# Spreading the p row by a VectorE transpose and DRAM instead of TensorE, with a reordered head and one GpSimd scaling at the end

## The chip, the cores and the metric

The kernel runs on one core of one Trainium2 chip. The metric is device time in microseconds (us), the median of repeated executions.

## The reference, cut to what matters

For each of 16 samples, x is 1024 x 256 (f32) and adj is a symmetric 0/1 matrix of 1024 x 1024 (int32). Two layers follow each other.

```
# layer 0: sigmoid attention on the edges, then residual and layer norm
e     = leaky(einsum('id,jd->ij', x * a0, x))          # symmetric in i, j
alpha = where(adj == 1, sigmoid(e), 0)
x     = layernorm(x + alpha @ x + bias)
# layer 1: exp attention on the edges, then residual and layer norm
H     = x @ W
s, d  = H @ a_src, H @ a_dst
e     = where(adj != 0, exp(-leaky(s[:, None] + d[None, :])), 0)
x     = layernorm(x + elu((e @ H) / rowsum(e)))
```

The reference also covers edge values 2 to 4; the kernel checks that there are none and has a general path behind that check, which these inputs do not take.

## The kernel before

All 16 samples go through one pass, `one_kind_pass`, sample b in slot b. A sample's 1024 rows are 8 tiles of 128. All matrix products are f32. An edge weight of layer 1 is min(adj, p[n] * q[m]) with p = exp(-0.8 s) and q = exp(-0.8 d), up to factors that are put into H and cancel in the division by the row sum. So the weights tile of row block m needs q as one number per partition and **p as a row of 1024 numbers that is the same on all 128 partitions**. `project` leaves p and q as columns (`pqs[b]`, tile number along the free axis); something has to turn p into rows.

The order of instructions on every engine is written out by hand (`tc.manual_schedule()`), so each engine runs its list in program order. A slot b, from 1 on, has three stretches on TensorE:

- strips (about 22 us): `strip(b, jt)`, scores of tile jt against the tiles from jt on (matmul L227), two tanh on ScalarE (L235, L236), their maximum on VectorE (L237); `finish` (L243, and a diagonal addition on GpSimd, L253), and the mirror images through DRAM (`dump` L259/L263, `gather` L267, `mask` L274). In between lie the projections of sample b - 1 (`project`, L405; exps on ScalarE L413 and L414, H on L415). At jt = 6 comes `share_p(b-1)`: p's columns are transposed by TensorE (L431), copied to SBUF by ScalarE (L433), written to a DRAM row (L435) and read back to all partitions (L437), both DMAs from GpSimd's queue.
- sum0 (about 28 us): `multiply0` (L342), 8 tiles of 16 matmuls; after each tile `end0` on VectorE (L352, L295, L297), and, at t = 2 to 7, ahead of that tile's `end0`, the weights of sample b - 1 (`weights`, L449): tiles 0 and 1 at t = 2, one each at t = 3 to 6, two at t = 7.
- sum1 (about 28 us): `sum1` (L456) for sample b - 1, 8 tiles of 16 matmuls; VectorE and ScalarE end each tile (`elu` L479 to L489, `add` L494 to L297).

The last sample has no later slot to hide in. Its projections are laid between the tiles of sum1 of sample 14, after t = 5 and after t = 6, and each half of p is spread by four TensorE transposes and a ScalarE copy (`spread_p`, L424, L425). Its first four sum1 tiles run side by side over m while its weights are made; the other tiles follow, the last one in two halves of its columns (L715). The layer norm of the last tiles ends the program; `scale1` (L325) applies it to tiles 3 to 5 on ScalarE, which also loads the table for a square root there (L666).

At the head, x of sample 0 comes in four pieces of two tiles (L94, from the queues of SyncE and ScalarE in turn), and GpSimd's queue issues adj of sample 0 in four pieces (L102; two row halves, first for columns 0 to 511), then x and adj of sample 1. `transpose_x` (L203) turns each piece of x by TensorE; VectorE and ScalarE copy it out and scale it (L207 to L211). Then come strips 0 and 1, each in two chunks of columns, `finish` and `mirror` (L282, L284), and sum0.

Of the kernel before, what the change touches and what calls it, by code (L numbers as in the profile page):

```python
# [18 lines left out]
P = 128  # L19
# [11 lines left out]
def one_kind_pass(  # L31
# [64 lines left out]
    def load_adj(b, g, columns=None):  # L96

        if (b, g) not in adjs:
            adjs[b, g] = two.tile([P, HT, N], BF16, tag=f"adj{g}", name=f"adj_{b}_{g}")
        columns = columns or slice(None)  # L100
        rows = adjT[b].rearrange("(t p) i -> p t i", p=P)[:, ts(g, HT), columns]
        nc.gpsimd.dma_start(adjs[b, g][:, :, columns], rows)  # L102
# [62 lines left out]
    pcol = ps_e.tile([P, HALF], F32, tag="e", name="pcol")[:, 0:ND]  # L165
    nc.tensor.transpose(pcol, arow, ident[0:ND, 0:ND])
    nc.scalar.copy(acol, pcol)
    power = const.tile([P, NT], F32, tag="power", name="power")
    nc.gpsimd.memset(power, -0.5)
    def make_Wx(c):  # L170
# [4 lines left out]
            nc.vector.tensor_reduce(Wx[:, c, s : s + 1], wprod, AX.X, ALU.add)  # L175


    xTs, xas, als, tbs, mirs = {}, {}, {}, {}, {}

    def new_xT(b):  # L180

# [12 lines left out]
    def transpose_x(b, g):  # L194

        if g == 0:
            new_xT(b)
            xas[b] = one.tile([P, ND, N], F32, tag="xa", name=f"xa_{b}")
        for c in range(ND):
            pool, tag = ((ps_t, "t"), (ps_acc, "acc"), (ps_acc if c else ps_e, "acc" if c else "e"), (ps_t, "t"))[g]  # L200
            pt = pool.tile([P, 2, P], F32, tag=tag, name=f"pxT_{b}_{g}_{c}")
            for t in range(2):
                nc.tensor.transpose(pt[:, t, :], xs[b][:, 2 * g + t, ts(c, P)], ident)  # L203
            flat = pt.rearrange("p t q -> p (t q)")
            xT, xa = xTs[b][:, c, ts(g, 2 * P)], xas[b][:, c, ts(g, 2 * P)]
            if c == 0:
                nc.vector.tensor_copy(xT, flat)  # L207
                nc.vector.tensor_scalar(xa, xT, acol[:, 0:1], None, ALU.mult)
            else:
                nc.scalar.copy(xT, flat)  # L210
                nc.scalar.mul(xa, flat, acol[:, 1:2])  # L211

    def strip(b, jt):


        if jt == 0:
            als[b] = one.tile([P, NT, N], F32, tag="al", name=f"al_{b}")
        width = N - jt * P
        tb = four.tile([P, N], F32, tag="tb", name=f"tb_{b}_{jt}")
        tbs[b, jt] = tb  # L220
        n_chunks = -(-width // HALF)
        per = -(-(width // P) // n_chunks) * P
        for n, o in enumerate(range(0, width, per)):
            w = min(per, width - o)
            pe = ps_e.tile([P, HALF], F32, tag="e", name=f"pe_{b}_{jt}_{n}")
            for c in range(ND):
                nc.tensor.matmul(  # L227
                    pe[:, 0:w],
                    lhsT=xTs[b][:, c, ts(jt, P)],
                    rhs=xas[b][:, c, ds(jt * P + o, w)],  # L230
                    start=(c == 0),
                    stop=(c == ND - 1),
                )
            low = two.tile([P, HALF], F32, tag="low", name=f"low_{b}_{jt}_{n}")
            nc.scalar.activation(tb[:, ds(o, w)], pe[:, 0:w], AF.Tanh, scale=0.5)  # L235
            nc.scalar.activation(low[:, 0:w], pe[:, 0:w], AF.Tanh, scale=0.5 * SLOPE)  # L236
            nc.vector.tensor_tensor(tb[:, ds(o, w)], tb[:, ds(o, w)], low[:, 0:w], ALU.max)  # L237

    def finish(b, jt, c0=0, c1=N):

# [150 lines left out]
    def project(b, t):  # L391

        if t == 0:
            if b < B - 1:
                H = one.tile([P, NT, D + 1], F32, tag="H", name=f"H_{b}")
                Hs[b] = [H[:, m, :] for m in range(NT)]
            else:
                Hs[b] = []
                for g in range(2):
                    H = two.tile([P, HT, D + 1], F32, tag=f"adj{g}", name=f"H_{b}_{g}")  # L400
                    Hs[b] += [H[:, m, :] for m in range(HT)]
            pqs[b] = small.tile([P, NT, 2], F32, tag="pq", name=f"pq_{b}")
# [11 lines left out]
        nc.scalar.activation(pqs[b][:, t, :], pt[:, 0:2], AF.Exp, scale=SLOPE - 1.0)  # L414
        nc.scalar.mul(Hs[b][t][:, 0:D], pt[:, 2:], w)  # L415

    def spread_p(b, g):

        if g == 0:
            p_bcs[b] = one.tile([P, N], F32, tag="p", name=f"p_{b}")  # L420
        pt = ps_t.tile([P, HT, P], F32, tag="t", name=f"pp_{b}_{g}")
        for t in range(HT):
            col = pqs[b][:, g * HT + t, 0:1]
            nc.tensor.transpose(pt[:, t, :], col.to_broadcast([P, P]), ident)  # L424
        nc.scalar.copy(p_bcs[b][:, ts(g, HALF)], pt.rearrange("p t q -> p (t q)"))  # L425

    def share_p(b):


        pt = ps_t.tile([P, HT, P], F32, tag="t", name=f"prow_{b}")[0:NT, 0, :]  # L430
        nc.tensor.transpose(pt, pqs[b][:, :, 0], ident)  # L431
        row = one.tile([NT, P], F32, tag="row", name=f"row_{b}")
        nc.scalar.copy(row, pt)  # L433
        p_row = dram.tile([N], F32, tag="p_row", name=f"p_row_{b}")
        nc.gpsimd.dma_start(p_row.rearrange("(t p) -> t p", p=P), row)  # L435
        p_bcs[b] = one.tile([P, N], F32, tag="p", name=f"p_{b}")
        nc.gpsimd.dma_start(p_bcs[b], p_row.partition_broadcast(P))  # L437

    def check_pq(b):
        near = small.tile([P, NT, 2], F32, tag="near", name=f"near_{b}")  # L440
# [4 lines left out]
    def weights(b, m):  # L445

        if m == 0:
            es[b] = one.tile([P, NT, N], F32, tag="ew" if b < B - 1 else "al", name=f"e_{b}")
        nc.vector.scalar_tensor_tensor(  # L449
            es[b][:, m, :], p_bcs[b], pqs[b][:, m, 1:2], adjs[b, m // HT][:, m % HT, :], ALU.mult, ALU.min  # L450
        )

    hs, ys, y_of, mv1s, r1s = {}, {}, {}, {}, {}

# [48 lines left out]
    def scale1(b, t):  # L503
        scale(ys[b][t], *r1s[b][t])
# [8 lines left out]

    for g in range(NT // 2):
        transpose_x(0, g)
    bias_bc = const.tile([P, D], F32, tag="bias", name="bias_bc")

    nc.vector.memset(bias_bc[:, 0:1], 0.0)  # L520
# [4 lines left out]
    nc.sync.dma_start(a_bc, a[0].partition_broadcast(P))  # L525
    Wx = const.tile([P, ND, D + 2], F32, tag="Wx", name="Wx")
    nc.sync.dma_start(Wx[:, :, 2:], W.rearrange("(c p) o -> p c o", p=P))
    strip(0, 0)
    strip(0, 1)
    for jt in range(2):  # L530
        finish(0, jt, 0, HALF)
        mirror(0, jt)
# [30 lines left out]
    for b in range(1, B):  # L563
# [58 lines left out]
        for t in range(NT):  # L622
            acc = acc1(prev, t, ps_acc, "acc")
            for m in range(NT):
                sum1(prev, t, acc, m)
            if last and t == 6:
                turn_x1(b, 1)
            if last and t == 7:
                weights(b, 0)
            elu(prev, t, acc)  # L630
            if last and t == 7:
                for m in range(1, 4):
                    weights(b, m)
            if t >= 1:
                add(prev, t - 1)
            if t == 0:
                fetch_x1(b, 0)
            if t in (1, 2):
                scale0(b, 2 * t + 2)
                scale0(b, 2 * t + 3)  # L640
            if t == 2:
                save_x1(b, 1)
            if t == 4:
                fetch_x1(b, 1)
                turn_x1(b, 0)
            if not last and t in (3, 5):
                turn_x(b + 1, (t - 3) // 2)
            if not last and t == 6:
                turn_x1(b, 1)
            if last and t in (5, 6):  # L650
                for n in range(HT):
                    project(b, (t - 5) * HT + n)
                spread_p(b, t - 5)
        if not last:
            add(prev, NT - 1)
            r1s[prev] = center(mv1s[prev], f"1_{prev}")
# [517 lines left out]
```

## Time and profile before

| | |
|---|---|
| median of 3 runs | 1272.78 us (1272.75 to 1272.94) |
| the profiled execution | 1273.82 us, of which the span in the trace is 1271.7 us |
| granted TensorE clock | 0.999 |
| PE busy | 1261.2 us, 99% of the span |
| DVE busy | 924.9 us, 73% |
| ACT busy | 651.4 us, 51% |
| POOL busy | 293.5 us, 23% |

PE is TensorE's matmuls, PEld its weight loads, DVE VectorE, ACT ScalarE, POOL GpSimd, SP SyncE; L431 is line 431 of the kernel before. The engines' busy times overlap. "out<-in" names the tile written and the tiles read. In the timeline a row is start, length, engine, line, operation, tiles, shape and count; instructions of one group that follow each other are merged into one row. A bracket at its end tells how long the engine was idle before it and on whom it waited. A DMA_DIRECT2D row on a queue is the issue of the transfer, not the transfer.

### The profile page before, as it was taken

The page shows a single profiled execution, that of the slowest core. Times are in us where ns is not written, and L with a number is a line of the kernel's source. Part 1 is how long each engine was busy: PE and PEld are TensorE (multiplying, and loading weights), DVE is VectorE, ACT ScalarE, POOL GpSimd, SP SyncE. Part 2 cuts the span into 40 slices and gives each one's busy share as a digit, 9 for nine tenths or more (in the row PEclk, how much of TensorE's full clock was granted, in tenths as well). Part 3 has the DMA queues.
Part 4 walks back from the last instruction along what each step waited for, and adds up shares of the span by engine and source line. Part 5 has one row for each costly group of instructions (what it writes and reads, how often), then busy time and mean ns, then how long its engine had stood idle before and what let it go on. Part 6 is the DMA issues. An engine that isn't in the chain of part 4 may idle for free.

```text
span 1271.7 us, 17514 instructions
## 1 busy us (share of the span) xinstructions
PE 1261.2 (99%) x5484; PEld 1025.7 (81%) x5484; DVE 924.9 (73%) x2017; ACT 651.4 (51%) x1469; POOL 293.5 (23%) x593
## 2 busy tenths in 40 slices
PE   9999999999999999999999999999999999999997
PEld 6788787887878878788787887878788787887886
DVE  5686867858678686786768868687686867868657
ACT  4644645456454564544645445454455645456434
POOL 2213231212312122121232212223112231212203
PEclk9999999999999999999999999999999999999999
DMA  9388595895949869497695966949579595895312
GB/s 219 67 174 143 103 188 96 176 181 101 194 88 180 168 117 200 77 183 154 130 194 92 182 133 139 209 83 182 117 168 188 95 190 97 174 181 103 99 34 69
DMA packets 603416, 180.24 MB, mean 142 GB/s; under 512 B 481722, under 2 KB 585652, under 8 KB 603316
## 3 DMA queue, kind: packets, MB, share of 16 engines
q1 hardware_dynamic: 581760, 135.85, 54.3%
q0 software_dynamic: 20864, 42.53, 18.6%
q8 instruction: 46, 0.75, 0.3%
q10 hardware_dynamic: 692, 0.66, 0.2%
q14 instruction: 54, 0.44, 0.1%
HBM read 151.91 MB, written 60.62 MB: 167 GB/s over the span
## 4 chain that ended last, share of the span: by engine, by line
PE 98%; DMA 1%; DVE 0%; ACT 0%; issue 0%; ACTq 0%; DVEq 0%
PE acc L342 35%; PE acc L456 35%; PE pe L227 19%; PE pH L405 9%; DMA x<-in_x 1%; PE pal L282 0%; PE prow L431 0%; PE pp L424 0%; ACT y L325 0%; ACT y_kept L325 0%; ACT L666 0%; PE px1T L388 0%; DVE y L494 0%; PE pxT L203 0%; ACTq L136 0%
## 5 line engine op out<-in xcount | busy, mean ns | idle before, releaser
L342 PE MATMUL acc<-x,al 128*128 128x256 f32 x2048 | 445.5, 379 | 0.0
L456 PE MATMUL acc<-H,e 128*128 128x257 f32 x2032 | 445.3, 380 | 0.0
L456 PEld LDWEIGHTS acc<-H,e 128*128 128x128 f32 x2032 | 384.8, 190 | 57.2 <-DVE e L449 0.6
L342 PEld LDWEIGHTS acc<-x,al 128*128 128x128 f32 x2048 | 387.7, 190 | 51.7
L227 PE MATMUL pe<-xa,xT 128*128 128x384 f32 (+1 forms) x720 | 250.9, 486 | 0.0
L227 PEld LDWEIGHTS pe<-xa,xT 128*128 128x128 f32 x720 | 132.7, 189 | 80.8 <-issue 43.1
L325 ACT ACTIVATE x<-x,mr,r 128x256 f32<-128x256 f32 x128 | 69.4, 592 | 227.8 <-POOL mr L321 227.8
L449 DVE SCALAR_TENSOR_TENSOR e<-p,pq,adj 128x1024 f32<-128x1024 f32 x128 | 159.7, 1269 | 29.2 <-DMA p<-p_row 26.1
L304 POOL TENSOR_SCALAR ve<-mv 128x4 f32<-128x4 f32 (+2 forms) x49 | 16.8, 343 | 657.0 <-DVE mv L297 652.9
L488 ACT ACTIVATE h<-acc,rinv 128x256 f32<-128x256 f32 x126 | 59.1, 469 | 203.4 <-DVE rinv L480 187.9
L235 ACT ACTIVATE tb<-pe 128x512 f32<-128x512 f32 (+1 forms) x192 | 94.1, 490 | 119.8 <-PE pe L227 94.6
L479 DVE TENSOR_SCALAR rinv<-acc 128x1 f32<-128x1 f32 x127 | 19.9, 157 | 161.2 <-PE acc L456 161.1
L237 DVE TENSOR_TENSOR tb<-tb,low 128x512 f32<-128x512 f32 (+1 forms) x192 | 103.3, 543 | 39.9 <-ACT low L236 39.8
L125 ACT ACTIVATE junk<-adj,minus 128x2048 bf16<-128x2048 bf16 x64 | 127.3, 1989 | 0.0
L405 PE MATMUL pH<-Wx,x1T 128*128 128x258 f32 x512 | 126.3, 381 | 0.0
L405 PEld LDWEIGHTS pH<-Wx,x1T 128*128 128x128 f32 x512 | 97.2, 190 | 35.8 <-issue 14.3
L253 POOL TENSOR_TENSOR al<-ident,al 128x128 f32<-128x128 f32 x128 | 67.0, 523 | 230.4 <-DVE al L243 229.9
L243 DVE SCALAR_TENSOR_TENSOR al<-tb,adj 128x512 f32<-128x512 f32 (+7 forms) x132 | 97.4, 739 | 5.3 <-DVE tb L237 0.4
L236 ACT ACTIVATE low<-pe 128x512 f32<-128x512 f32 (+1 forms) x192 | 93.2, 485 | 0.5 <-DVE tb L237 0.5
L274 DVE SCALAR_TENSOR_TENSOR al<-al,adj 128x512 f32<-128x512 f32 (+3 forms) x150 | 77.3, 539 | 19.7 <-DMA al<-mir 19.6
L352 DVE SCALAR_TENSOR_TENSOR x<-acc,bias_bc 128x256 f32<-128x256 f32 x128 | 53.7, 420 | 41.5 <-PE acc L342 41.5
L259 DVE STREAM_TRANSPOSE tb<-tb 128x896 f32<-128x896 f32 (+6 forms) x105 | 74.7, 712 | 3.6
(108 smaller groups left out, 950.1 us busy)
## 6 DMA issues: line engine op xcount, KB each, us to landing
adj<-in_adjT POOLq DMA_DIRECT2D x30, 1024.0 KB, 10.3
x_rows<-x SPq DMA_DIRECT2D x31, 512.0 KB, 4.6
x1T<-x_rows SPq DMA_DIRECT2D x248, 64.0 KB, 2.5
out<-y_kept SPq DMA_DIRECT2D x30, 512.0 KB, 6.8
x<-in_x SPq DMA_DIRECT2D x14, 1024.0 KB, 6.1
xT<-in_x SPq DMA_DIRECT2D x112, 128.0 KB, 4.7
p<-p_row POOLq DMA_DIRECT2D x15, 512.0 KB, 4.5
mir<-tb SPq DMA_DIRECT2D x60, 112.0 KB, 3.0
```

The costliest lines, as they stand in the source:

```text
L125: nc.scalar.activation(junk, rows, AF.Square, bias=minus1, scale=2.0, accum_out=chk[:, b * CHECKS + n : b * CHECKS + n + 1],)
L227: nc.tensor.matmul(pe[:, 0:w], lhsT=xTs[b][:, c, ts(jt, P)], rhs=xas[b][:, c, ds(jt * P + o, w)], start=(c == 0), stop=(c == ND - 1),)
L235: nc.scalar.activation(tb[:, ds(o, w)], pe[:, 0:w], AF.Tanh, scale=0.5)
L236: nc.scalar.activation(low[:, 0:w], pe[:, 0:w], AF.Tanh, scale=0.5 * SLOPE)
L237: nc.vector.tensor_tensor(tb[:, ds(o, w)], tb[:, ds(o, w)], low[:, 0:w], ALU.max)
L243: nc.vector.scalar_tensor_tensor(als[b][:, jt, c0:c1], tbs[b, jt][:, c0 - jt * P : c1 - jt * P], 1.0, adjs[b, jt // HT][:, jt % HT, c0:c1] ...
L259: nc.vector.transpose(tb, tb)
L274: nc.vector.scalar_tensor_tensor(v, v, 1.0, rows, ALU.add, ALU.mult)
L342: nc.tensor.matmul(acc, lhsT=als[b][:, jt, ts(t, P)], rhs=xs[b][:, jt, :], start=(jt == 0), stop=(jt == NT - 1),)
L405: nc.tensor.matmul(pt, lhsT=x1Ts[b][:, c, ts(t, P)], rhs=Wx[:, c, :], start=(c == 0), stop=(c == ND - 1),)
L449: nc.vector.scalar_tensor_tensor(es[b][:, m, :], p_bcs[b], pqs[b][:, m, 1:2], adjs[b, m // HT][:, m % HT, :], ALU.mult, ALU.min)
L456: nc.tensor.matmul(acc, lhsT=es[b][:, m, ts(t, P)], rhs=Hs[b][m], start=(m == 0), stop=(m == NT - 1),)
```

## The change

- `spread_p` goes. `share_p` now transposes p's columns on VectorE: p and q live in one constant tile `pq_kept` of 128 x 32 (zeroed once), p in columns 0 to 7 and q in 8 to 15, and VectorE's 32 x 32 block transpose writes `pT`. For samples 0 to 14 one DMA writes all of pT (128 rows of 128 B) to DRAM and one reads it back to all partitions, as four runs of 1 KB for each partition. The p row then has its blocks in the order (i, t, j) in place of (t, i, j).
- `weights` for samples 0 to 14 is therefore four instructions of 128 x 256 for each row block, in place of one of 128 x 1024; the adj and e operands are read and written in runs of 32 elements.
- For sample 15 the projections come after t = 4 and t = 6, its first x1 half is turned at t = 3 in place of t = 4, and p goes through DRAM in halves of 512 columns: for each half four writes of 4 x 128 B and one broadcast. Its weights are made in halves of the columns, the first halves before and between the first four m, the second halves from m = 5 on.
- The first adj DMA is held until the first piece of x has come, by a one-element copy from x into adj's tile on GpSimd.
- At the head, the product of strip 0's first chunk goes between the third and the fourth transposed piece of x; the other chunks' products and tanh steps are reordered.
- The scaling of tile 4 of the last sample goes from ScalarE to GpSimd.

```diff
 # load_adj
             adjs[b, g] = two.tile([P, HT, N], BF16, ...)
+            if (b, g) == (0, 0):
+                nc.gpsimd.tensor_copy(adjs[b, g][:, 0, 0:1], xs[b][:, 0, 0:1])
...
+    pq_kept = const.tile([P, SQ], F32, tag="pq", name="pq_kept")
+    nc.gpsimd.memset(pq_kept, 0.0)
...
 # project
-            pqs[b] = small.tile([P, NT, 2], F32, tag="pq", name=f"pq_{b}")
+            pqs[b] = pq_kept[:, 0 : 2 * NT].rearrange("p (k t) -> p k t", k=2)
...
-    def spread_p(b, g):
...
+    def share_p(b, t0=0, n=NT):
+        if t0 == 0:
+            p_bcs[b] = one.tile([P, P // SQ, NT, SQ] if b < B - 1 else [P, N], F32, ...)
+        pT = one.tile([P, SQ], F32, tag="pT", name=f"pT_{b}_{t0}")
+        nc.vector.transpose(pT, pq_kept)
+        if b < B - 1:
+            p_row = dram.tile([P // SQ, SQ, SQ], F32, tag="p_row", name=f"p_row_{b}")
+            nc.gpsimd.dma_start(p_row.rearrange("i t j -> (i t) j"), pT)
+            nc.gpsimd.dma_start(p_bcs[b], p_row[:, 0:NT, :].partition_broadcast(P))
+        else:
+            p_row = dram.tile([n * P], F32, tag="p_end", name=f"p_row_{b}_{t0}")
+            v = p_row.rearrange("(t i j) -> i t j", i=P // SQ, j=SQ)
+            for i in range(P // SQ):
+                nc.gpsimd.dma_start(v[i], pT[ds(i * SQ + t0, n), :])
+            nc.gpsimd.dma_start(p_bcs[b][:, ds(t0 * P, n * P)], p_row.partition_broadcast(P))
...
 # weights(b, m, t0=0, n=NT), cols = ds(t0 * P, n * P)
-        nc.vector.scalar_tensor_tensor(
-            es[b][:, m, :], p_bcs[b], pqs[b][:, m, 1:2], adjs[b, m // HT][:, m % HT, :], ALU.mult, ALU.min
-        )
+        if b < B - 1:
+            e, rows = [v.rearrange("p (t i j) -> p i t j", i=P // SQ, j=SQ) for v in (e, rows)]
+            for i in range(P // SQ):
+                nc.vector.scalar_tensor_tensor(e[:, i], p_bcs[b][:, i], q, rows[:, i], ALU.mult, ALU.min)
+        else:
+            nc.vector.scalar_tensor_tensor(e, p_bcs[b][:, cols], q, rows, ALU.mult, ALU.min)
...
 # head
-    for g in range(NT // 2):
+    for g in range(3):
         transpose_x(0, g)
+    score(0, 0, 0)
+    transpose_x(0, 3)
...
-    strip(0, 0)
-    strip(0, 1)
+    for jt, n in ((1, 0), (0, 1)):
+        score(0, jt, n)
+    for jt, n in ((0, 0), (1, 0), (0, 1)):
+        squash(0, jt, n)
+    score(0, 1, 1)
+    squash(0, 1, 1)
...
 # sum1 of sample 14, tile t (last), around elu(prev, t, acc)
+            if last and t == 3:
+                turn_x1(b, 0)
             if last and t == 7:
-                weights(b, 0)
+                for m in range(2):
+                    weights(b, m, 0, HT)
             elu(prev, t, acc)
             if last and t == 7:
-                for m in range(1, 4):
-                    weights(b, m)
+                for m in range(2, 6):
+                    weights(b, m, 0, HT)
...
-            if last and t in (5, 6):
+            if last and t in (4, 6):
+                t0 = (t - 4) // 2 * HT
                 for n in range(HT):
-                    project(b, (t - 5) * HT + n)
-                spread_p(b, t - 5)
+                    project(b, t0 + n)
+                share_p(b, t0, HT)
...
 # the first four sum1 tiles of sample 15, step m
-        if m >= 4:
-            weights(last, m)
-        if m == 5:
+        if m in (3, 4):
+            weights(last, m + 3, 0, HT)
+        if m == 4:
             add(done, NT - 1)
             r1s[done] = center(mv1s[done], f"1_{done}")
+        for k in range(3 * m - 15, min(3 * m - 12, NT)) if m >= 5 else []:
+            weights(last, k, HT, HT)
...
 # the end
+    y, (r, mr) = ys[last][4], r1s[last][4]
+    nc.gpsimd.tensor_scalar(y, y, r, mr, ALU.mult, ALU.add)
     scale1(last, 3)
-    scale1(last, 4)
```

`strip` is split into `score` (the matmuls) and `squash` (two tanh and the maximum); in all other places it calls both in the old order.

More of the change, by code (lines that the diff above doesn't have):

```diff
@@ L175, in make_Wx @@
             nc.vector.tensor_reduce(Wx[:, c, s : s + 1], wprod, AX.X, ALU.add)
-    xTs, xas, als, tbs, mirs = {}, {}, {}, {}, {}
+    xTs, xas, als, tbs, pes, mirs = {}, {}, {}, {}, {}, {}
     def new_xT(b):
@@ L217, in strip, with chunks, score, squash @@
             als[b] = one.tile([P, NT, N], F32, tag="al", name=f"al_{b}")
+        tbs[b, jt] = four.tile([P, N], F32, tag="tb", name=f"tb_{b}_{jt}")
+        for n in range(len(chunks(jt))):
+            score(b, jt, n)
+            squash(b, jt, n)
+    def chunks(jt):
         width = N - jt * P
-        tb = four.tile([P, N], F32, tag="tb", name=f"tb_{b}_{jt}")
-        tbs[b, jt] = tb
         n_chunks = -(-width // HALF)
         per = -(-(width // P) // n_chunks) * P
[L223 to L232, printed above, removed]
-                )
[L234 to L237, printed above, removed]
+        return [(o, min(per, width - o)) for o in range(0, width, per)]
+    def score(b, jt, n):
+        o, w = chunks(jt)[n]
+        pe = pes[jt, n] = ps_e.tile([P, HALF], F32, tag="e", name=f"pe_{b}_{jt}_{n}")
+        for c in range(ND):
+            nc.tensor.matmul(
+                pe[:, 0:w],
+                lhsT=xTs[b][:, c, ts(jt, P)],
+                rhs=xas[b][:, c, ds(jt * P + o, w)],
+                start=(c == 0),
+                stop=(c == ND - 1),
+            )
+    def squash(b, jt, n):
+        o, w = chunks(jt)[n]
+        tb, pe = tbs[b, jt][:, ds(o, w)], pes[jt, n][:, 0:w]
+        low = two.tile([P, HALF], F32, tag="low", name=f"low_{b}_{jt}_{n}")[:, 0:w]
+        nc.scalar.activation(tb, pe, AF.Tanh, scale=0.5)
+        nc.scalar.activation(low, pe, AF.Tanh, scale=0.5 * SLOPE)
+        nc.vector.tensor_tensor(tb, tb, low, ALU.max)
     def finish(b, jt, c0=0, c1=N):
@@ L413, in project @@
         nc.scalar.activation(w, pt[:, 1:2], AF.Exp, scale=-SLOPE)
-        nc.scalar.activation(pqs[b][:, t, :], pt[:, 0:2], AF.Exp, scale=SLOPE - 1.0)
+        nc.scalar.activation(pqs[b][:, :, t], pt[:, 0:2], AF.Exp, scale=SLOPE - 1.0)
         nc.scalar.mul(Hs[b][t][:, 0:D], pt[:, 2:], w)
-    def spread_p(b, g):
[L419 to L437, printed above, removed]
+    def share_p(b, t0=0, n=NT):
+        if t0 == 0:
+            p_bcs[b] = one.tile([P, P // SQ, NT, SQ] if b < B - 1 else [P, N], F32, tag="p", name=f"p_{b}")
+        pT = one.tile([P, SQ], F32, tag="pT", name=f"pT_{b}_{t0}")
[10 more added lines that the diff above has]
+            nc.gpsimd.dma_start(p_bcs[b][:, ds(t0 * P, n * P)], p_row.partition_broadcast(P))
@@ L439, in check_pq @@
     def check_pq(b):
-        near = small.tile([P, NT, 2], F32, tag="near", name=f"near_{b}")
+        near = small.tile([P, 2, NT], F32, tag="near", name=f"near_{b}")
         nc.vector.tensor_scalar(near, pqs[b], LOW, 1.0 / LOW, ALU.max, ALU.min)
@@ L443, in check_pq, with weights @@
         nc.vector.tensor_reduce(fit[:, b : b + 1], near, AX.XY, ALU.min)
-    def weights(b, m):
-        if m == 0:
+    def weights(b, m, t0=0, n=NT):
+        if m == 0 and t0 == 0:
             es[b] = one.tile([P, NT, N], F32, tag="ew" if b < B - 1 else "al", name=f"e_{b}")
-        nc.vector.scalar_tensor_tensor(
-            es[b][:, m, :], p_bcs[b], pqs[b][:, m, 1:2], adjs[b, m // HT][:, m % HT, :], ALU.mult, ALU.min
-        )
+        cols = ds(t0 * P, n * P)
+        q, e, rows = pqs[b][:, 1, m : m + 1], es[b][:, m, cols], adjs[b, m // HT][:, m % HT, cols]
+        if b < B - 1:
[4 more added lines that the diff above has]
+            nc.vector.scalar_tensor_tensor(e, p_bcs[b][:, cols], q, rows, ALU.mult, ALU.min)
     hs, ys, y_of, mv1s, r1s = {}, {}, {}, {}, {}
@@ L511, in acc1 @@
         return pool.tile([P, D + 1], F32, tag=tag, name=f"acc1_{b}_{t}")
-    for g in range(NT // 2):
+    for g in range(3):
         transpose_x(0, g)
+    als[0] = one.tile([P, NT, N], F32, tag="al", name="al_0")
+    for jt in range(2):
+        tbs[0, jt] = four.tile([P, N], F32, tag="tb", name=f"tb_0_{jt}")
+    score(0, 0, 0)
+    transpose_x(0, 3)
     bias_bc = const.tile([P, D], F32, tag="bias", name="bias_bc")
@@ L644, in one_kind_pass @@
                 fetch_x1(b, 1)
-                turn_x1(b, 0)
+                if not last:
+                    turn_x1(b, 0)
             if not last and t in (3, 5):
```

## The prediction

> **What bounds the kernel.** I read the page's chain of waits first, then the chain in order of time, then VectorE's timeline in a middle slot, then head and end. The chain is TensorE's own work almost throughout, at a granted clock of 0.999; in the chain in order of time (start, length), piece follows piece, the transposition of p (L431) among them.
>
> ```profile
> PE 98%; DMA 1%; DVE 0%; ACT 0%; issue 0%; ACTq 0%; DVEq 0%
> ```
> ```profile
> 623.57 0.86 PE pe L227 x4
> 624.44 0.11 PE prow L431
> 624.55 0.45 PE pe L227 x4
> 624.99 27.63 PE acc L342 x128
> ```
>
> So a middle slot gets shorter by what leaves TensorE, if nothing else becomes late there. The one candidate is VectorE, which makes sample 7's weights (L449) in slot 8 beside sum0 (timeline; last brackets are waits):
>
> ```profile
> 644.61 1.25 DVE L449 SCALAR_TENSOR_TENSOR e<-p,pq,adj 128x1024 f32<-128x1024 f32 x1
> 645.78 0.42 DVE L352 SCALAR_TENSOR_TENSOR x<-acc,bias_bc 128x256 f32<-128x256 f32 x1
> ...
> 646.79 1.25 DVE L449 SCALAR_TENSOR_TENSOR e<-p,pq,adj 128x1024 f32<-128x1024 f32 x1
> 649.21 0.42 DVE L352 SCALAR_TENSOR_TENSOR x<-acc,bias_bc 128x256 f32<-128x256 f32 x1 [1.16 <-PE acc L342]
> ...
> 650.23 2.45 DVE L449 SCALAR_TENSOR_TENSOR e<-p,pq,adj 128x1024 f32<-128x1024 f32 x2
> 652.66 0.42 DVE L352 SCALAR_TENSOR_TENSOR x<-acc,bias_bc 128x256 f32<-128x256 f32 x1
> ```
>
> From p's arrival at 636.30 on VectorE has no pause but this 1.16; the weights end at 652.68. At the head and at the end there are waits on the path (TensorE for x's fourth piece; VectorE, then bound by its own work, for TensorE):
>
> ```profile
> 8.44 0.41 PE L203 MATMUL pxT<-ident,x 128*128 128x128 f32 x2 [1.61 <-DMA x<-in_x]
> ```
> ```profile
> 1256.51 0.16 DVE L479 TENSOR_SCALAR rinv<-acc 128x1 f32<-128x1 f32 x1 [0.28 <-PE acc L456]
> ...
> 1260.31 0.16 DVE L479 TENSOR_SCALAR rinv<-acc 128x1 f32<-128x1 f32 x1 [0.46 <-PE acc L456]
> ```
>
> **Slots 1 to 15: what is removed.** One transposition a slot, 0.11 us in the chain: 15 x 0.107 = **1.6 us**. ScalarE's copy (0.24) was off the path.
>
> **Slots 1 to 15: what is added.** (1) A VectorE transposition of 128x32 after `dump(b, 6)`. L259 takes 0.31 at 128 columns and 0.13 for each further 128, so about 0.2. VectorE reached this place at 626.7 in slot 8 and p's exps were ready at 623.9, so it waits for nothing. Behind it are `mask` 1 and the rest of the strips; VectorE still pauses 0.59 for TensorE at 631.94 and for p until 636.30, which absorb 0.2. (2) On GpSimd's queue the write of p starts after that transposition, 627.0 in place of 626.89, now in 128 rows of 128 B; the read in 512 runs of 1 KB in place of 128 of 4 KB. Nearest rows: p_row landed in 2.5 to 4.6 us (median 3.1), mir<-tb, whose runs are of 128 B too, in 3.5 at 16 KB, x_rows<-x, runs of 1 KB, in 4.6 at 512 KB beside 4.5 for p. So p comes 0.1 to 1.5 us later; I take 0.3, since the rows of like runs are no slower. The Trainium skill, "DMA: Bandwidth & Descriptors", Specifications, warns that transfers under 512 B are read, modified and written; it names no price for one so small. GpSimd waits between the two DMAs as before, and the diagonal of strip 7 behind it is wanted only by the last sum0 tile.
>
> (3) `weights` becomes 4 instructions of 128x256 for one of 128x1024. No row shows 256 columns with a per-partition scalar. L243, the same operation with a constant, takes 0.424 at 256 and 1.225 at 1024; L449 takes 1.269 at 1024, so I expect 0.47 at 256. Two L449 start 1.20 apart and are 1.25 long, so some 0.07 overlaps: 0.40 from start to start. Bounds: 0.333, the distance of three independent L284 at 128x256 (1.08 in all, 0.416 each), and 0.47 with no overlap. A row block costs 4 x 0.40 - 1.20 = **0.40 more** (0.13 to 0.67). The middle value lies nearest to the row of the same line.
>
> The Trainium skill, "VectorE: DVE Perf Modes", section on the TRN2 errata, speaks against this: every SBUF-source instruction pays a fixed cost (58 cycles in its table, about 151 measured), so it advises 512 elements or more. By its two figures, an estimate, a row block would cost 0.18 or 0.47 more, and with 0.47 slots 1 and 8 would stall by 0.35 us each, 0.7 us on the sum. The trace bears the rule out in kind: L449 has a fixed part of about 0.2 us beside its columns.
>
> What hides it: six row blocks come before `end0` of tile 6, two after it. TensorE needs the eighth in sum1's first tile: that starts at 652.46, its m = 7 comes 7 x 0.435 later at 655.5, the weight load 0.2 earlier, 655.3. With the semaphore I allow 655.15: 2.47 after the old end. Together with the 1.2 pause, slot 8 has 3.7 us; needed are 8 x 0.40 + 0.3 = 3.5. In the other slots I measured the same pauses ahead of `end0` of tiles 4 to 6: 1.24 (slot 1, too) up to 3.6, mean 2.2, because p arrives 8.9 to 11.3 us after sum0's start. So **no stall, but only just**: slots 1 and 8 have 0.2 us left, the mean slot 1.2. What comes behind is covered: VectorE pauses 2.4 us before the first sum1 tile's L479, and adj's next load and x1's save move by up to 3 us with margins larger than that (adj lands in 10 us, wanted 25 later).
>
> **Sample 15.** `spread_p` goes twice: 0.65 us each in TensorE's row (1223.36 to 1224.00), 1.3 us with its waits for ScalarE. TensorE's first four tiles start at 1233.7 in place of 1235.1. p's first half: exps at 1220.3 (3.48 earlier, one tile), VectorE 0.2, four write issues of at most 0.64 (L435), landing 3.1 after the last, then 4.95 as from the old read's issue to VectorE's start: 1230.6 (at most 1232). Its user `weights` 0 runs on VectorE after the second transposition (1230.8); TensorE wants it at 1233.5, so nothing is late. Second half: 1240.8 (to 1242.5), while VectorE reaches it at 1241.1: after L479/480 (1234.15), four halves at 0.67, one `add` (1.48), two halves, one `add`. Then eight halves: 1246.5, and the checks to 1247.55, where the old order ended at 1247.9 and then waited until 1248.25. So VectorE starts the final chain 0.7 earlier, and its waits of 0.28 and 0.46 on TensorE vanish partly, since TensorE is now 1.4 ahead: about **1.0**. If p's second half is 1 us late, 0.3 is left; if all waits go, 1.4. `turn_x1` of the second half ends at 1226.3 by this count, TensorE wants it at 1226.6: 0 to 0.3 lost, taken as 0.
>
> **The last scaling.** ScalarE did tiles 3 and 4 in 1.08 from 1263.24, and the last exp (L739) started at 1264.42 although its input was there at 1264.06; the square root's table load follows at 1264.81. Without tile 4: about **0.35** earlier (0 to 0.5). GpSimd is free from 1263.0 and needs about 1 us by L147 (0.56 at 128 columns), beside ScalarE's tile 3; the store is then issued no later than before.
>
> **The head.** TensorE finishes 12 transpositions at 6.83, then waits. Strip 0's first chunk (1.72) fits there as soon as ScalarE's scaled copy is ready at 7.18: 7.1 to 8.8. Then the fourth piece, whose x now comes without adj beside it (it landed at 8.3; the rate had fallen from 385 to 150 GB/s after 5 us), then three products: TensorE ends the strips at 14.0, in place of 15.35. But `mirror` 0 needs the tanh of strip 0's second chunk, and that product now comes third: TensorE 12.7, tanh pair to 14.0, maximum to 14.8, so `mirror` starts at 14.95: **0.45** gained (0 to 1.4). Held adj: the first piece lay ready at 1.88 and now waits for x at 3.65, so four issues, x of sample 1 and sample 1's adj behind it move by 2.2 us. The first two pieces landed at 10.8 and 13.4; wanted at about 15.8 and 17 by L243 and L284. Even the full shift holds.
>
> **Sum.** 1.6 + 1.0 + 0.35 + 0.45 = 3.4. The profiled execution takes 1273.82 with a span of 1271.7; the span goes to 1268.3, the median from 1272.78 to **1269.4 us**. A measurement of this kernel can tell about 0.2%, 2.5 us, from no change; so faster means under 1270.2, slower over 1275.3.
>
> **Rivals.**
> A, the gain is swallowed at the two ends: p's second half comes late, `mirror` waits, and slots 1 and 8 stall by some tenths. Then the 1.6 of L431 remain: 1271.2. For it: my margins of 0.3 in p's halves; against: they count every DMA at the old size. 0.24.
>
> B, slower: VectorE becomes the bound in sum0. Place: the eighth row block ahead of sum1's first tile. Price: with 0.47 a quarter and p 0.3 late, 6 x 0.67 + 0.3 = 4.3 less the pause, plus 2 x 0.67 - 2.47: 1.95 in slots 1 and 8, 1.0 in the mean slot, 15 us in all, less 3.4: 1284.5. It decides from 0.435 a quarter on, where the stalls, some 3.5 us, eat the gain. For it: runs of 32 elements, which no row shows; against: L284 at 0.333 with runs of 128. 0.20.
>
> C, the change does less than it says: TensorE's gap at L431 is filled by a wait of the following strip for ScalarE, so only the end and the head bring anything: 1271. Against it: L227 follows L405 without a gap elsewhere. 0.03, counted with A.
>
> My forecast has 0.53.
>
> **Range.** 1267.8 (head 1.4, end 1.9, slots 1.6, a little rounding) to 1277 (B in its milder half, 0.45 a quarter, with p 1 us late); likeliest alone 1268 to 1270.2. Faster 0.53, same 0.27, slower 0.20.
>
> **What would show it.** Right: L431 and L424 gone, the start of sum0 moved by 0.11 a slot, L449's quarters 0.40 apart, p arriving 9 to 11.6 us after sum0's start, no wait of PEld for L449 in slots 1 to 15, VectorE without pause from 1247 to the last L479, sum0's first tile 0.45 earlier. Wrong: PEld L456 waiting on L449 by about 1 us a slot (B); a TensorE wait at `mirror` 0 of over 1.4, or VectorE waiting on p in sample 15 (A).

## The result, and the profile after

The change made the kernel slower: 1275.43 us (1273.55 to 1278.6, 18 runs) against 1272.70 us (1271.92 to 1277.29, 18 runs) for the kernel before, a ratio of 1.002 [1.0014, 1.0027]. The forecast was 1269.4 us and faster. The time lies inside the range, in the part that belonged to rival B, on the side that had 0.20.

The chain of waits of the changed kernel, by engine, where before TensorE had 98%:

```profile
PE 67%; DVE 11%; DMA 6%; issue 1%; ACT 1%; SPq 1%; POOL 0%; DVEq 0%; ACTq 0%; POOLq 0%
```

The path now leaves TensorE for VectorE and the DMA engines. Where it leaves is seen in slot 8 of the chain in order of time (start, length, piece):

```profile
628.19 0.14 DVE pT L441
628.33 0.99 DVE al L291 x2
629.32 0.07 issue
629.39 2.81 DMA p_row<-pT
632.24 0.52 issue
632.76 6.67 DMA p<-p_row
639.45 3.26 DVE e L468 x8
...
654.55 3.15 DVE e L468 x8
657.75 25.06 PE acc L475 x114
```

p's write, p's read, the weights of sample 7 in quarters (L468) and then sum1 (L475) follow each other without a pause. Three more views of the changed kernel show the two sides of it: VectorE's timeline in that slot, TensorE's weight loads there, and the issues of DMA (queue, count, size, median us to landing).

```profile
634.18 0.56 DVE L291 SCALAR_TENSOR_TENSOR al<-al,adj 128x384 f32<-128x384 f32 x1
639.45 3.26 DVE L468 SCALAR_TENSOR_TENSOR e<-p,pq_kept,adj 128x256 f32<-128x256 f32 x8 [4.72 <-DMA p<-p_row]
...
654.46 3.23 DVE L468 SCALAR_TENSOR_TENSOR e<-p,pq_kept,adj 128x256 f32<-128x256 f32 x8
```
```profile
656.16 0.30 PEld L475 LDWEIGHTS acc<-H,e 128*128 128x128 f32 x2 [0.23 <-DVE e L468]
657.74 4.43 PEld L475 LDWEIGHTS acc<-H,e 128*128 128x128 f32 x21 [1.29 <-DVE e L468]
```
```profile
p<-p_row POOLq DMA_DIRECT2D x15, 512.0 KB, 6.1
```

The same row of the kernel before:

```profile
p<-p_row POOLq DMA_DIRECT2D x15, 512.0 KB, 4.5
```

sum0 starts at 625.86 in this slot, so p is there 13.59 us after it. VectorE sits idle for 4.72 us ahead of p and has no pause behind it; TensorE then waits 1.29 for the last row block. The read of p lands in 6.1 us, before in 4.5.

Two times describe a slot: from sum0's start (its first product) to p's first use, which is the start of the first row block, and the slot's length (sum0's start to the next one's). Before, every slot is 78.04 long. After, it is 77.93 (0.11 less, as L431's place in the chain said) unless p comes late:

| slot of the changed kernel | 4 | 13 | 2 | 3 | 6 | 8 | 12 |
|---|---|---|---|---|---|---|---|
| p after sum0's start, us | 11.90 | 11.37 | 12.75 | 12.59 | 14.31 | 13.59 | 13.35 |
| longer than 77.93 by, us | 0 | 0 | 0.47 | 0.31 | 2.02 | 1.31 | 1.07 |

The excess is p's time less 12.28 in each of the five that are longer. The mean of p's time over slots 1 to 15 is 12.27 after and 10.48 before. Its parts: the write's issue 2.57 (before 2.10), write to read 3.66 (3.84), read to first row block 6.04 (4.54).

The span of the profiled execution goes from 1271.7 to 1273.8 us. The pieces: sum0 of sample 0 starts at 18.47 in place of 19.35, -0.89. From there to slot 1 -0.11. Slots 1 to 14 take 1096.18 in place of 1092.56: 14 x 0.11 less and 5.2 of stalls, +3.62. From sum0's start in slot 15 to the issue of the last store 96.57 in place of 97.06, with another stall of 0.75 in it, -0.49. The stretch from that issue to the end of the span 3.46 in place of 3.56, -0.10. Together +2.0.

### The profile page after: what moved, and what is told of

It is laid out like the page before. It is cut to its first block, busy times and chain, and to the rows that moved or that the text cites. A ratio compares the mean times of both kernels' runs of the same rounds, so it can differ in the third digit from the quotient of the medians.

```text
span 1273.8 us, 17899 instructions
## 1 busy us (share of the span) xinstructions
PE 1259.7 (99%) x5461; PEld 1023.6 (80%) x5461; DVE 967.0 (76%) x2402; ACT 647.6 (51%) x1451; POOL 278.7 (22%) x606
## 4 chain that ended last, share of the span: by engine, by line
PE 67%; DVE 11%; DMA 6%; issue 1%; ACT 1%; SPq 1%; POOL 0%; DVEq 0%; ACTq 0%; POOLq 0%
PE acc L475 30%; PE acc L359 17%; PE pe L240 13%; PE pH L422 6%; DVE e L468 6%; DMA p<-p_row 3%; DMA p_row<-pT 1%; DVE st L312 1%; DMA al<-mir 1%; DVE x L369 1%; DMA mir<-tb 1%; SPq L280 1%; DVE al L260 1%; DVE tb L254 1%; DVE mv L314 1%
## 5 line engine op out<-in xcount | busy, mean ns | idle before, releaser
L475 PE MATMUL acc<-H,e 128*128 128x257 f32 x2032 | 446.7, 380 | 3.3 <-DVE e L468 3.3
L475 PEld LDWEIGHTS acc<-H,e 128*128 128x128 f32 x2032 | 384.4, 190 | 62.4 <-DVE e L468 6.2
L468 DVE SCALAR_TENSOR_TENSOR e<-p,pq_kept,adj 128x256 f32<-128x256 f32 x480 | 196.4, 477 | 52.4 <-DMA p<-p_row 52.4
L342 ACT ACTIVATE y_kept<-y_kept,mr,r 128x256 f32<-128x256 f32 x120 | 64.9, 592 | 1.1 <-DVE y L513 1.1
```

The lines of the kernel that those rows point to most:

```text
L342: nc.scalar.activation(y, y, AF.Identity, bias=mr, scale=r)
L468: nc.vector.scalar_tensor_tensor(e[:, i], p_bcs[b][:, i], q, rows[:, i], ALU.mult, ALU.min)
L475: nc.tensor.matmul(acc, lhsT=es[b][:, m, ts(t, P)], rhs=Hs[b][m], start=(m == 0), stop=(m == NT - 1),)
```

## The experiments

My theory after these views: p is late by 1.8 us and the row blocks longer by 8 x 0.4, and only both together use up the 3.7 us of slack that the prediction had found. The rivals: the quarters alone do it; the collision of p's read with the load of the next sample's x does it; the changed ends do it.

**The change without the new way of p in slots 1 to 15** (label no_mid: head, hold and end as changed; there TensorE's transposition and whole row blocks).

```diff
-        nc.vector.transpose(pT, pq_kept)          # samples 0 to 14
...
+            nc.tensor.transpose(pt, pqs[b][:, 0, :], ident)
...
+            nc.scalar.copy(row, pt)
...
+            nc.gpsimd.dma_start(p_row.rearrange("(t p) -> t p", p=P), row)
+            nc.gpsimd.dma_start(p_bcs[b], p_row.partition_broadcast(P))
```

> The changed kernel with the old way of p in slots 1 to 15 (TensorE transposition, one read in runs of 4 KB, one instruction of 128x1024 a row block); head and end stay changed. Theory R (the loss sits in slots 1 to 15, where p comes late and the quarters take the rest of the slack): slots of 78.04 us again, no wait of PEld for the weights, and what head (0.9) and end (1.2) gained: 1270.6 us. Rival H (head or end lose, and the slots only look longer): 1274 or more.

Measured 1272.46 us (1272.03 to 1273.27), against 1273.02 before in that session, 0.9993 [0.9984, 1.0002]. All slots are 78.04 again. So the loss sits in slots 1 to 15. Head and end together bring 0.6 us by the clock, not the 1.8 of the prediction, and the interval does not exclude that they bring nothing.

**Quarters alone** (quart_only: the kernel before, with row blocks in four instructions of 256 columns).

```diff
...
+        for i in range(P // SQ):
+            nc.vector.scalar_tensor_tensor(e[:, i], pv[:, i], pqs[b][:, m, 1:2], rows[:, i], ALU.mult, ALU.min)
```

> The kernel before with one edit: the row blocks of samples 0 to 14 in four quarters with runs of 32 elements; p comes as before. Theory R: 8 x 0.39 = 3.1 is under the slack of 3.7 to 6 us, weights end 28 to 30.4 after sum0's start, no PEld wait, 1272.7 us. Rival Q (the quarters alone are enough): PEld waits for the weights in slots 1 and 8 at least, 1274 or more.

Measured 1272.61 us (1271.92 to 1275.19), 0.9998 [0.999, 1.0007]. The costliest groups of its page (busy and mean ns, then idle before and on whom) have the same quarters as the changed kernel, and half its wait for p:

```profile
L459 DVE SCALAR_TENSOR_TENSOR e<-p,pq,adj 128x256 f32<-128x256 f32 x480 | 196.4, 477 | 24.0 <-DMA p<-p_row 24.0
```

The same group in the changed kernel, and the whole row blocks of the kernel before (all 16 samples):

```profile
L468 DVE SCALAR_TENSOR_TENSOR e<-p,pq_kept,adj 128x256 f32<-128x256 f32 x480 | 196.4, 477 | 52.4 <-DMA p<-p_row 52.4
```
```profile
L449 DVE SCALAR_TENSOR_TENSOR e<-p,pq,adj 128x1024 f32<-128x1024 f32 x128 | 159.7, 1269 | 29.2 <-DMA p<-p_row 26.1
```

With p at 10.64 on average the quarters lengthen no slot: all are 78.04.

**p in natural order** (nat_one: the changed kernel, with p written in four DMAs, read in runs of 4 KB, row blocks whole; nat_quart: the same with quarters).

```diff
-            nc.gpsimd.dma_start(p_row.rearrange("i t j -> (i t) j"), pT)
-            nc.gpsimd.dma_start(p_bcs[b], p_row[:, 0:NT, :].partition_broadcast(P))
...
+            for i in range(P // SQ):
+                nc.gpsimd.dma_start(v[i], pT[ds(i * SQ, NT), :])
+            nc.gpsimd.dma_start(p_bcs[b], p_row.partition_broadcast(P))
```

> The changed kernel with p written to DRAM in natural order by four small DMAs in place of one, so that the read has runs of 4 KB and each row block is one instruction again; still no TensorE transposition. Theory R: p arrives some 12 us after sum0's start (the four issues cost 1.5), but without the quarters the weights end at 27.9 to 28.5 after it, under the 30.6 at which TensorE wants them: slots of 77.93, 1269.0 us. Rival M (a late p alone is enough for the stalls): slots 6, 8 and 12 stall again, 1273 or more.

> As nat_one (four writes, read in runs of 4 KB) but the row blocks in four quarters with runs of 32 elements. Theory R: p some 12 us after sum0's start, as late as in the changed kernel, and 8 x 0.39 for the quarters: stalls by max(0, 6 x 0.39 + delay of p - pause) + 0.78 - 2.47 a slot, so 1274 to 1276 us, with weights ending past 30.6 in several slots. Rival T (only the 1 KB runs of the read hurt): 1269 to 1270.

Both missed: 1276.95 us (1275.23 to 1278.63), 1.003 [1.002, 1.004], and 1282.03 us (1278.24 to 1285.02), 1.007 [1.0053, 1.0088]. In nat_one every slot is 77.92 or 77.93 but slot 10, which is 82.67 long. Its timeline, SP's and GpSimd's DMA issues and then VectorE and TensorE:

```profile
787.98 0.43 SPq L94 DMA_DIRECT2D x<-in_x  x1
788.42 0.57 POOL L447 DMA_DIRECT2D p<-p_row  x1 [4.95 <-issue]
788.52 10.90 SPq L120 DMA_DIRECT2D xT<-in_x  x8
796.15 2.48 DVE L468 SCALAR_TENSOR_TENSOR e<-p,pq_kept,adj 128x1024 f32<-128x1024 f32 x2 [8.69 <-DMA p<-p_row]
799.02 11.23 PE L359 MATMUL acc<-x,al 128*128 128x256 f32 x43 [2.79 <-DVE x L369]
```

The read was issued 0.4 us behind the load of the next sample's x (1 MB and eight pieces of 128 KB) and took 7.7 us. VectorE stood in its queue waiting for p, so sum0's own tiles waited for VectorE. TensorE's wait of 2.79 is only a part of the 4.74 us lost: the granted clock is 0.86 in the 12.31 us from there to the end of sum0, and the 48 products left would take 10.4 at the pace of the sum0 that the prediction shows (27.63 for 128). Four write issues in place of one had moved the read from 6.2 to 7.4 us after sum0's start (in this slot to 9.6), where x's load can come first. The expectations left out what else is issued there.

In nat_quart, slot 10 has the same collision: p comes at 17.55, TensorE waits 3.76 and then has a clock of 0.86 for 12.31 us, and the slot is 5.72 longer than 77.93, more than p less 12.28. Slots 7, 8 and 11, with p at 12.39, 13.60 and 12.70, are 0.10, 1.32 and 0.41 longer, which is p less 12.28.

**x's load held until p has come** (after_holdx: the changed kernel with the hold; nat_holdx: nat_one with it).

```diff
+            nc.gpsimd.tensor_copy(xs[b][:, 0, 0:1], hold[:, 0:1])   # hold = p_bcs of the sample before
```

> The changed kernel with one edit: the load of the next sample's x is held until p has come. Theory R: r->p stays at 5.4 to 6.7 (runs of 1 KB), weights end at 29.3 to 31.6 after sum0's start, the stalls of 0.3 to 1.3 us in some slots stay, only one like that of slot 6 (2.0 us, x's load issued ahead of p's landing) goes: 1273.5 to 1275. Rival X: r->p falls to about 5, no stalls, 1271.

> The changed kernel with p in its natural order (four writes, a read in runs of 4 KB, one instruction a row block), and the load of the next sample's x held until p has come, by a copy of one element on GpSimd. Rival X applied to this variant (what cost 4.7 us in one slot was the read of p behind x's 1 MB): r->p 4.5 to 5.0 in every slot, no slot over 78.0, 1270.5 to 1271.3. If the collision was not the cause: slots of 79 to 83 us as without the hold, 1275 to 1277. If the held x comes too late for its transpositions in the same slot: every slot longer by the same amount, 0.3 us or more, 1277 and up.

after_holdx took 1273.38 us (1271.82 to 1276.5), 1.0001 [0.999, 1.0011]. The slot of 79.95 is gone, but slots 2, 3, 8, 9 and 12 are 0.4 to 0.8 longer than 77.93, slot 15 has p at 14.23, and the read to the first row block takes 6.26 on average. In the changed kernel's profile that slot, slot 6, is the only one where x's load is issued ahead of p's landing. So the collision is a part, about 2 us between two sessions, and not what makes the read slow. In nat_holdx all slots are 77.92 or 77.93, the read to the first row block is 4.25: the collision was the cause in slot 10 of nat_one. Its time is 1273.86 us (1273.34 to 1274.52) all the same, because the stretch from the last store's issue to the end of the span is 7.5 us there, and 3.5 in the changed kernel. What makes it longer stayed open.

**The length of the runs** (runs: the kernel before, p read into a tile with gaps, in runs of 4 KB, 1 KB, 2 KB or 512 B by sample; k4_quart: runs of 1 KB, and quarters).

```diff
...
+        flat = one.tile([P, N + 64], F32, tag="p", name=f"p_{b}")
+        p_bcs[b] = flat[:, 0 : k * (N // k + 8)].rearrange("p (k n) -> p k n", k=k)[:, :, 0 : N // k]
+        nc.gpsimd.dma_start(p_bcs[b], p_row.rearrange("(k n) -> k n", k=k).partition_broadcast(P))
```

> The kernel before, with one edit: the read of p is cut into runs of 4 KB, 1 KB, 2 KB or 512 B per partition, by sample in turn; the write, the transposition and the one-instruction row block stay. Theory R (the length of the runs sets the landing): from the read's issue to VectorE's first row block 4.5 to 4.9 us at 4 KB, about 5.2 at 2 KB, 6.0 at 1 KB and 7 or more at 512 B, slot after slot. Rival X (the read is late because it shares the DMA engines with the load of the next sample's x, whatever its runs): 4.5 to 5.1 at every length, and single slots of 7 or more where x's load was issued before p had landed. By both, no slot over 78.1 us, since a row block of one instruction leaves 3.7 us: 1272.6 in all.

> The kernel before, with p read in four runs of 1 KB and a row block in four instructions of 256 contiguous columns; TensorE's transposition, ScalarE's copy, the write in rows of 512 B, the head and the end are those of before. Theory R: p lands 6.0 us after the read's issue, at 11.9 after sum0's start in the mean slot; eight row blocks cost 8 x 0.39 more; with 2.47 + 1.24 us of slack several slots stall by 0.2 to 2 us, some 3 us in all: 1275 to 1276. Rival X: p lands in 4.8, no stall outside of a slot with a collision: 1272.6. Rival Q (the quarters' 32-element runs cost something that shows only with a permuted p): 1272.6, too, since here the columns are contiguous.

From the read's issue to the first row block the slots of one length average 4.81 (4 KB), 4.80 (2 KB), 5.06 (1 KB) and 6.20 us (512 B; 5.82 to p's landing, since VectorE came 1.1 later than p in one of the three slots). No slot of runs is over 78.04, and its one execution took 1272.60 us. Runs of 1 KB cost 0.25, not the 1.5 of the changed kernel; k4_quart has 4.96 with 1 KB in every slot, no stall, and 1273.12 us, 1.0001 [0.9992, 1.001]. My theory fell in that form: short runs in SBUF are not it. But here the gaps were in SBUF, and in the changed kernel they are in DRAM: p_row has 32 x 32 elements for each i, of which 8 x 32 are read, so the four pieces lie 4 KB apart.

**The distance in DRAM** (src_gap: the kernel before, whole row blocks, p_row in four pieces of 1 KB at four distances by sample).

```diff
+        gap = (N // 4, N, N // 4 + 32, N + 32)[b % 4]
...
+        p_row = p_row.rearrange("(k n) -> k n", k=4)[:, 0 : N // 4]
+        for i in range(2):
+            nc.gpsimd.dma_start(p_row[:, ts(i, P)], row[i :: 2, :])
```

> The kernel before, with p_row laid out in DRAM as four pieces of 1 KB, by sample in turn: contiguous, 4096 B apart, 1152 B apart, 4224 B apart; written by two DMAs, read by one, into a tile without gaps; row blocks stay one instruction. Theory S (the changed kernel's read is late because its source in DRAM lies in four pieces 4 KB apart): from the read's issue to the first row block 4.5 to 5.0 us in the contiguous slots, 5.7 to 6.3 at 4096 B; if the distance decides, 1152 B stays near 5.0. Rival W (what delays is that p_row was just written in pieces of 128 B): 4.5 to 5.0 at every layout. No slot over 78.1 us by either, since whole row blocks leave 3.7 us: 1272.6.

| distance of the 1 KB pieces | 1024 B (no gap) | 1152 B | 4224 B | 4096 B |
|---|---|---|---|---|
| read's issue to first row block, mean of 3 or 4 slots, us | 4.52 | 4.68 | 6.37 | 7.22 |

Two slots side by side, 4224 B apart (slot 4) and without a gap (slot 5), GpSimd's and VectorE's rows of one timeline:

```profile
317.57 0.80 POOL L440 DMA_DIRECT2D p<-p_row  x1 [3.47 <-DMA p_row<-row]
323.73 2.48 DVE L452 SCALAR_TENSOR_TENSOR e<-p,pq,adj 128x1024 f32<-128x1024 f32 x2 [3.63 <-DMA p<-p_row]
...
395.72 0.56 POOL L440 DMA_DIRECT2D p<-p_row  x1 [3.58 <-DMA p_row<-row]
400.26 2.48 DVE L452 SCALAR_TENSOR_TENSOR e<-p,pq,adj 128x1024 f32<-128x1024 f32 x2 [2.72 <-DMA p<-p_row]
```

Issue to use is 6.16 in the one and 4.54 in the other. Two of the four slots at 4096 B had x's load ahead of p's landing; the other two have 6.88 and 6.53. So pieces that lie 4 KB apart make the read 1.9 to 2.2 us slower by themselves; a gap of 128 B costs 0.2. No slot is over 78.05: with whole row blocks a p at 14.25 stalls nothing, and the one execution took 1271.88 us.

**Both together, nothing else of the change** (gap_quart: the kernel before, 4096 B apart in every sample, and quarters).

> The kernel before with two edits: p_row in four pieces of 1 KB that lie 4096 B apart in DRAM (every sample), and a row block in four instructions of 256 columns; TensorE's transposition, ScalarE's copy, head and end are those of before. Theory S (distance in DRAM plus quarters make the loss, neither alone): p comes 12.5 to 14.3 us after sum0's start, and a slot is longer than 78.04 by what p is later than 12.3 (in the changed kernel slots 2, 3, 6, 8 and 12 had p at 12.75, 12.59, 14.31, 13.59, 13.35 and were 0.47, 0.31, 2.02, 1.31, 1.07 longer): about 1 us in the mean slot, 10 to 20 us in all, 1282 to 1292. Rival (DVE's transposition, the 128 B rows of the write or the changed ends are needed for the loss): slots of 78.04, 1272.6.

Measured 1281.28 us (1279.81 to 1282.82), 1.0069 [1.0055, 1.0082]; a little under the expected range, since p came at 12.59 on average. TensorE's weight loads in slot 6:

```profile
498.68 0.30 PEld L467 LDWEIGHTS acc<-H,e 128*128 128x128 f32 x2 [0.22 <-DVE e L462]
500.27 2.91 PEld L467 LDWEIGHTS acc<-H,e 128*128 128x128 f32 x14 [1.29 <-DVE e L462]
```

This is the same pair of waits as in slot 8 of the changed kernel. Nine of the slots 1 to 14 have p later than 12.28 and are longer than 78.04, together by 7.3 us. In slots 2, 6, 9 and 12, for instance, p came at 12.70, 14.05, 13.15 and 13.66, and they are 0.42, 1.77, 0.86 and 1.38 longer: p less 12.28 again, as in the other five. Neither VectorE's transposition nor the 128 B rows of the write nor the ends are needed for the loss. The opposite test is missing: no run takes only the distance in DRAM out of the changed kernel, and the variants without it also write p in four DMAs.

**The ends by themselves** (end_only: the kernel before with the changed end; head_order: no_mid without the hold of adj).

> The kernel before with the changed end alone (p of sample 15 in two halves through DRAM, last scaling of tile 4 on GpSimd); head and slots 1 to 14 as before. Theory E (the end brings what was reckoned): from sum0's start of slot 15 to the issue of the last store 95.8 us in place of 97.1, the time 1271.3 to 1271.6. If the stretch behind the last store takes some of it back (3.9 in place of 3.5 us, as with the changed head and end together): 1271.8 to 1272.4.

> The changed head and end, the old p in slots 1 to 15, and adj's first load not held. Theory: the hold buys a steady head (sum0's start 18.4 to 18.7 us in every kernel with the new head, 18.0 to 19.8 with the old one); without it x's fourth piece comes beside adj again, sum0 starts at 18.5 to 19.5, 1272.5 to 1273.2 with a wide spread. Rival: only the order matters, the hold does nothing: 18.45, 1272.4 to 1272.6 with the narrow spread of the held version (1272.03 to 1273.27).

end_only took 1271.91 us (1271.19 to 1275.59) against 1272.57 before, 0.9996 [0.9987, 1.0005]. From sum0's start in slot 15 to the last store's issue it has 95.86 us, before 97.06: the end brings 1.2. Its span is 1.1 shorter by the median (1269.4 against 1270.5), and 0.3 of it is lost outside of the span (time less span 2.4 against 2.1). The clock shows 0.7, and its interval includes no change. head_order took 1272.57 us (1272.35 to 1273.05), with sum0 at 18.51: in the new head the hold of adj does nothing that can be measured.

**A version that beats both** (nat_act: nat_holdx with two of the four writes of p on ScalarE's queue; near_quart: the same queues and the hold, p in the changed order without gaps, quarters).

```diff
-                nc.gpsimd.dma_start(v[i], pT[ds(i * SQ, NT), :])
+                (nc.gpsimd, nc.scalar)[i % 2].dma_start(v[i], pT[ds(i * SQ, NT), :])
```

> The variant with p in natural order and the held x, with two of the four writes of p on ScalarE's queue in place of GpSimd's. Two issues a queue in place of four: write to read 3.9 to 4.2 us (5.06 before), p 1 us earlier at 10.8, every slot 77.93. The stretch from the last store's issue to the end of the span was 7.6 us in that variant against 3.5 in the changed kernel: if it goes with the number of GpSimd's DMAs it falls to about 5 and the time to 1271 to 1272; if not, 1273.9.

> The changed kernel with p_row written without gaps (four writes, two on GpSimd's and two on ScalarE's queue), read in runs of 4 KB, and x's load held; the quarters of 256 columns stay. p comes at 11.0 to 13.2 as in the variant with whole row blocks on the same queues (mean 12.15). By the rule of 12.3 some five slots stall by 0.3 to 0.9, 2 to 3 us in all: 1272.5 to 1273.5, against 1270.36 with whole row blocks. If quarters are free once the read has no gaps: 1270.4.

nat_act took 1270.36 us (1269.95 to 1270.59) against 1272.57, 0.9982 [0.9973, 0.9991]. Its chain of waits:

```profile
PE 97%; DVE 2%; ACT 1%; issue 0%; ACTq 0%; DVEq 0%
```

All slots are 77.92 or 77.93, although the first row block starts at 12.15 on average. Write to read fell from 5.06 to 3.00 (from GpSimd's first write), but read to first row block rose from 4.25 to 6.67. Only 1.0 of this rise is the read (4.23 to 5.28 until p has landed). The other 1.4 is a wait for something else: in all 15 slots VectorE stands ahead of the row blocks in `mask`, waiting for a mirror image (al<-mir), while p is there already. The last `mask` starts at 11.7 us after sum0's start on average, in nat_holdx at 8.3; what makes the mirror image later is not shown. In slot 2, VectorE's rows and then GpSimd's copy that waits for p:

```profile
166.93 0.56 DVE L293 SCALAR_TENSOR_TENSOR al<-al,adj 128x384 f32<-128x384 f32 x1 [3.11 <-DMA al<-mir]
167.40 2.48 DVE L470 SCALAR_TENSOR_TENSOR e<-p,pq_kept,adj 128x1024 f32<-128x1024 f32 x2
...
166.14 0.18 POOL L92 COPY x<-p 128x1 f32<-128x1 f32 x1 [4.69 <-DMA p<-p_row]
```

The Trainium skill, "DMA: Bandwidth & Descriptors", section "Issuing engines are not separate DMA queues", says that transfers issued by several engines share the same 16 DMA engines, and that only issue time is saved; these numbers agree in kind: between p's issue and its landing the packets of the queues of SyncE and ScalarE keep the DMA engines 0.51 busy in nat_act and 0.22 in nat_holdx (mean of 15 slots). The stretch from the last store's issue to the end of the span is 4.1. near_quart took 1273.31 us (1271.35 to 1275.25), 1.0001 [0.9992, 1.001]: in its slots 3, 4, 5 and 11 the first row block started at 13.11, 12.84, 13.56 and 13.58, and they were 0.82, 0.55, 1.27 and 1.29 longer (slots 8 and 14, at 12.51 and 12.56, by 0.22 and 0.27). Here, too, it is the mirror image that VectorE waits for in all 15 slots; p landed 1.2 to 1.6 us ahead of the row block. So the threshold is one on the start of the row blocks, whatever delays it.

## Why the prediction was wrong, point by point

- **p's lateness is the term that failed.** The prediction took 0.3 us for it, with 1.5 as the upper bound; the mean is 1.79, and in slot 6 p came at 14.31. The read alone is 1.50 of it. The prediction weighed the read by the length of its runs, with x_rows (runs of 1 KB) as the nearest row. On the length of the runs that is nearly right (0.25 us by the experiment on run lengths). But x_rows is a store from SBUF to DRAM, not a read, and the new read differed in another way: its source lay in pieces 4 KB apart, which the change's text showed (32 x 32 written, 8 x 32 read). The two further parts: the write's issue 0.47 later in place of 0.1, the write itself 0.2 faster. On that write the prediction quoted the Trainium skill's warning on transfers under 512 B; write to read was 3.66 us with rows of 128 B and 3.84 with 512 B, so no price shows here.
- **The price of a quarter was right.** 0.40 from start to start was predicted; eight take 3.26, (3.26 - 0.48) / 7 = 0.40. A row block costs 0.39 more. Of the two figures that the prediction worked out from the Trainium skill, "VectorE: DVE Perf Modes", section on the TRN2 errata (0.18 and 0.47 more), this lies nearer to the larger.
- **The slack and the stall formula were right to 0.3 us.** The prediction left 0.2 us in slot 8 with p 0.3 late. Counted from sum0's first product as here, p came at 11.47 before, so that is a stall from 12.0 on; it begins at 12.28. With p's measured times the formula puts stalls in the same six slots, each 0.3 too long. "No stall, but only just" was the sentence to distrust: an answer that hangs on 0.2 us with a bound of 1.5 on one term is not a likeliest case at 0.53.
- **Rival B had the right place and the wrong cause.** TensorE waits for the last row blocks of the weights in sum1's first tile, as B said, but quarters of 0.47 were not what brought it there, and 5.9 us of stalls in 6 slots is less than its 15. That the time lies inside the range is partly luck: the upper end was reckoned with 0.45 a quarter, which did not come.
- **L431 brought what was reckoned**: 0.11 a slot, 1.6 in all.
- **The end was nearly right**: 1.0 + 0.35 predicted, 1.2 measured from slot 15 to the last store.
- **The head was right in kind and nothing in time.** Against the profile shown, sum0 starts 0.89 earlier. But in seven profiles with the old head it starts at 17.52 to 19.78, mean 18.52, as x's fourth piece comes early or late; in eight with the new head and the hold at 18.12 to 18.70, mean 18.45. The profile of before, at 19.35, was one with a late piece: a wait for x of 1.0 to 1.6 us, as shown in the prediction with 1.61, is in three of the seven, and none is in the other four, which start at 17.86 on average. The new head is steadier and hardly earlier on average, and later than an old head whose piece came in time.

So the sum that the runs support is -1.6 (L431) - 1.2 (end) - 0 (head) + 5.9 (stalls), +3.1, and the clock shows +2.7.

## What to carry to other kernels

When a transfer is put into another layout, compare source and destination apart, distance by distance, with rows that have the same gaps on the same side; a row with equal run lengths is not yet a like row. Where two costs draw on one slack, give the case in which both are at their upper half its own price and chance, and measure the slack as a threshold (here the first row block at 12.28 us after sum0's start), because it then gave the stalls of every variant with quarters, but for the one slot (slot 10 of nat_quart) where the granted clock fell as well. It is no threshold for whole row blocks. A wait that one profiled execution shows at the start may be a draw of a lottery: compare several profiles before subtracting it.

## What the runs showed of the hardware

- A broadcast read of 4 KB to 128 partitions, from four pieces of 1 KB in DRAM: 4.5 us to first use with no gap, 4.7 at a distance of 1152 B, 6.4 at 4224 B and 7.2 at 4096 B (6.9 and 6.5 in the two slots without the load of x ahead). Single reads scatter: with 4096 B in every slot (gap_quart) they take 5.05 to 7.90. With the gaps in SBUF instead and none in DRAM: 4.8 at runs of 4 KB, 5.1 at 1 KB and 6.2 at 512 B. Whether it is the distance in DRAM as such or a boundary of some size in between was not tried. The Trainium skill, "DMA: Bandwidth & Descriptors", section "Latency and other measured facts", reports copies between tensors in HBM that slow down with the row pitch, from 207 GB/s at 512 KiB to 103 at 4 MiB, where 192 B more per row did not help and 4 KiB more did. No run here had such a pitch; whether the effect at 4 KB is the same one is not shown.
- A small read issued 0.4 us behind the load of 1 MB landed in 7.7 us (nat_one; in nat_quart, 0.9 behind it, in 8.3), in place of 4.2 on average with that load held. Because its user stood at the head of VectorE's queue, TensorE lost 4.7.
- After TensorE's waits of 2.79 us (nat_one) and 3.76 us (nat_quart) in slot 10, the granted clock was 0.86 over the next 12.31 us, which cost another 1.9 us; after the wait of 1.29 us in slot 8 of the changed kernel it stayed at 1.00.
- The stretch from the last store's issue to the end of the time differed between programs, by the profiled runs: 5.6 us before and after, 6.1 to 6.5 in the three variants with the old p in slots 1 to 15 and the new end, 7.3 in nat_one and nat_quart, 9.3 in nat_holdx, 5.9 in nat_act. The cause stays open.
